# Filling the block-diagonal keys by transfers instead of masked copies, in a four-layer transformer kernel on one core

## The chip, the cores and the metric

The kernel runs on one core of one Trainium2 chip. Its time is the device time of one launch in microseconds (us); the figure that counts is the median of several runs. The engines are named as in the profile: PE multiplies matrices, PEld loads its weights, DVE, ACT and POOL work elementwise, SP issues DMAs.

## The reference, cut to what matters

There are 128 sequences of 64 tokens with 128 channels, a condition vector for each sequence and a context of 64 tokens for each sequence. All is float32. Attention has 16 heads of 8 channels.

```python
x = x + g_sa * (attend(ln(x) * (1 + sc) + sh) @ sa_proj_w + b)     # layer 0, self attention:  L0s
x = x + attend(q=ln(x), kv=context) @ ca_proj_w + b                # layer 0, cross attention: L0c
x = x + g_ff * mlp(ln(x) * (1 + sc_ff) + sh_ff)                    # MLP of layer 0
x = x + attend(q=ada_ln(x, c), kv=ada_ln(context, c)) @ Wp + bp    # layer 1, cross attention: L1c
x = x + gate_a * (attend(ln(x) * (1 + s) + t) @ W_proj + b)        # layer 2, self attention:  L2s
x = x + attend(q=ln(x), kv=ln(context)) @ W_cproj + b              # layer 2, cross attention: L2c
x = x + gate_m * mlp(...)                                          # MLP of layer 2
x = x + sigmoid(...) * (sum_e prob_e * expert_e(...) @ out_w + b)  # layer 3: one head, router, three experts
# attend: per sequence and head softmax(q k^T / sqrt(8)) v, with q, k, v projections and biases
```

## The kernel before, in words

The sequences are cut into 16 groups of 8 (512 tokens). The x of all groups stays in SBUF. Five attention layers of 16 groups each, 80 groups in all, go through one software pipeline, `attend`; MLPs and layer 3 have their own.

**Heads inside one matmul.** `prepare` (line 386) makes for each group qT and kT, both 128 channels x 512 tokens. A head has 8 channels, and PE multiplies 32 rows at a time: 4 heads share 32 rows. So that one query row block meets the keys of each head alone, the keys are spread into `kbd` (128 x 4 x 8 x 64): slice j holds the keys of the j-th head of each four and zeros elsewhere. Lines 443 to 446 make it with four POOL instructions, kT times a 0/1 mask column. `scores` (line 468) multiplies qT with kbd into `sc`, takes the maximum (`mx`, L485) and subtracts it (`e`, L487), both on DVE. `turned` (line 493) transposes on PE (`pp`, L503), and ACT takes the exponential on the way out (`eT`, L507).

**Values, sums and o.** `vbd` holds for each pair of heads the 16 value columns of the pair and two columns of ones among 32, so that `weighted` (line 509, `po`, L520) gives values and softmax sums in one multiplication. The result `o` has 128 rows: per 32 rows, 16 of values and two of sums, and two free-axis halves (even and odd pairs).

**finish** (line 530), for each group in four pieces: (0) SP stores the sum rows to DRAM in two DMAs (`sums`), loads them spread over 128 partitions (`rc`), and folds the second half of o into rows 16 to 31 of each 32 with four DMAs (`o<-o`); (1) DVE takes the reciprocal, SP stores it (`recs`), loads the gate tile (`gt`, self attention only, two DMAs from a table in DRAM with 1 KB rows) and the reciprocals repeated over 8 rows each (`rb`, one DMA); (2) POOL multiplies `oT = o * rb` and adds the bias to x; (3) PE projects (`py`, L563), and the result goes into x.

**The order is written by hand.** `step(k)` handles one half group: scores of the present half, `turned` of the last, `weighted` of the one before, with pieces of `prepare` and `finish` between. Each engine runs its instructions in that order, and each waits in place. For group i the keys are made (piece 5 of `prepare`) in the first half of group i-1 and used at the start of group i. `reciprocal`, `recs`, `gt` and `rb` of group i-2 are issued in the first half of group i, before the context load of group i+4 (`c`, L394).

SP issues nearly all DMAs in program order; at the start these are x and all weights.

Of the kernel before, what the change touches and what calls it, by code (L numbers as in the profile page):

```python
# [9 lines left out]
F32 = mybir.dt.float32  # L10
AF = mybir.ActivationFunctionType
ALU = mybir.AluOpType
# [23 lines left out]
for _name, _n in _VECS:  # L36
# [15 lines left out]
}  # L52
_RAW = [
    "x", "cond_1024", "ctx_1024", *_WTS,
    "L0_xcond_ca_proj_b", "L1_xcond_bp", "L2_xcond_b_cproj", "L3_xcond_router_b", "L3_xcond_e_b2",
# [4 lines left out]
def tile_kernel(ctx: ExitStack, tc: tile.TileContext, a: dict, out: bass.AP):  # L60
# [5 lines left out]
    def const(shape, name):  # L66
        return cp.tile(shape, F32, tag=name, name=name)
# [11 lines left out]
    mask = const([P, 4], "mask")  # L79
    nc.scalar.dma_start(mask, a["mask"])  # L80

    w = {}

    def load_weights(prefix, pool=cp):
        for name, (k, n) in _WTS.items():
            if name.startswith(prefix):
                t = pool.tile([P, k, n], F32, tag=name, name=name)
                src = a[name]
                if len(src.shape) == 3:
                    src = src.rearrange("e c n -> (e c) n")  # L90
                nc.sync.dma_start(t, src.rearrange("(k p) n -> p k n", p=P))
                w[name] = t

    xs = [const([P, TT, P], f"x{s}") for s in range(NST)]
# [23 lines left out]

    ident = const([P, P], "ident")
    make_identity(nc, ident)  # L120
    nhalf = const([P, TT], "nhalf")
    G.memset(nhalf, -0.5)

# [37 lines left out]
    def mm(name):  # L161
        return pools[1].tile([P, 512], F32, tag="mm", name=name)
# [4 lines left out]
        Places.ak.tile([P, NB, 8, 32], F32, tag=f"vbd{i}", name=f"vbd{i}", bufs=1) for i in range(2)  # L167
    ]

    def clear(t):  # L170
        G.memset(t, 0.0)
        G.memset(t[0:L, :, :, 16:17], 1.0)
        G.memset(t[L:P, :, :, 17:18], 1.0)


# [2 lines left out]
    condT = const([P, P], "condT")  # L178
    scT = const([P, P], "scT")
    mods = {}  # L180

    def col(name, i=0):
        r = _ROW[name] + i
        return vec[:, r : r + 1]
# [19 lines left out]

    def folded_column(wp, bp, bv, i):
        pb = mm("pb")
        T.matmul(pb[:, 0:1], w[wp][:, 0], col(bv, i), start=True, stop=True)
        t = const([P, 1], "pb_" + wp)
        V.tensor_add(t, pb[:, 0:1], col(bp))
        proj_bias[wp] = t  # L210
# [3 lines left out]
    def gate_table(wmod, wp, i=2, bias=None):  # L214

        table = dp.tile([P, 2, P], F32, tag="gate_" + wp, name="gate_" + wp)
        rows = const([P, 2, P], "gate_rows")
        gb = const([P, P], "gate_bias")
        V.tensor_scalar_mul(gb, mods[wmod][:, i, :], proj_bias[wp] if bias is None else bias)

        def second():
            pg = mm("pg")
            for q, src in enumerate((mods[wmod][:, i, :], gb)):
                T.transpose(pg[:, ts(q, P)], src, ident)
            V.tensor_copy(rows, pg[:, 0 : 2 * P].rearrange("p (i c) -> p i c", i=2))
            nc.sync.dma_start(table, rows)
            gates[wp] = table

        return second

    def folded_row(wp, bp, bv):
        bvs = const([P, P], "bvs")
        V.tensor_copy(bvs, col(bv, 1).broadcast_to([P, P]))

        def second():
            pb = mm("pb")
            T.matmul(pb[:, :P], bvs, w[wp][:, 0], start=True, stop=True)
            V.tensor_add(row_bias[bp], row_bias[bp], pb[:, :P])
            proj_bias[wp] = row_bias[bp]

        return second

    def condition():
        pc = mm("pc")
        T.transpose(pc[:, :P], cond, ident)
        V.tensor_copy(condT, pc[:, :P])
        S.activation(scT, pc[:, :P], AF.Silu)
        pv = mm("pv")
        T.transpose(pv[:, :_NVEC], vec_rows, ident[:_NVEC, :_NVEC])
        V.tensor_copy(vec, pv[:, :_NVEC])  # L250
        V.tensor_scalar_add(vec1, vec, 1.0)

    first_mods = modulations("L0_xcond_adaln_w", "L0_xcond_adaln_b", 6, (1, 4))
# [19 lines left out]
    def gate_tile(pool, s, wp):  # L273

        gt = pool.tile([P, TT, 2, P], F32, tag="gt", name="gt")
        for h in range(2):
            r = gates[wp].rearrange("(s t h) i c -> s h t (i c)", t=TT, h=2)[s, h]
            nc.sync.dma_start(
                gt[ts(h, L)].rearrange("p t i c -> p t (i c)"),
                r.unsqueeze(0).broadcast_to([L, TT, 2 * P]),  # L280
            )
        return gt

# [15 lines left out]
    def by_batch(t):  # L299
        return t.rearrange("p (b l) -> p b l", b=NB)  # L300
# [80 lines left out]

    turn = [0]

    ctxT = dp.tile([NST, P, NT], F32, tag="ctxT", name="ctxT")

    def prepare(pools, at):
# [52 lines left out]
        i = turn[0] % 2  # L439
        turn[0] += 1  # L440
        vbd = vbds[i]
        kbd = pool.tile([P, 4, NB, L], F32, tag="kbd", name="kbd")
        for j in range(4):
            (V if at.get("first") else G).tensor_scalar(  # L444
                kbd[:, j], by_batch(kT), mask[:, j : j + 1], 1.0, ALU.mult, ALU.mult
            )
        yield
        pq = psum.tile([P, 512], F32, tag="mm", name="pq")
        T.matmul(pq, at["wq"], q_in, start=True, stop=True)  # L449
# [11 lines left out]
                    start=True, stop=True,  # L461
                )
        pv4 = pvv.rearrange("p b (i d) -> p b i d", d=HD)
        S.copy(vbd[0:L, :, :, 0:HD], pv4[0:L])
        S.copy(vbd[L:P, :, :, HD : 2 * HD], pv4[L:P])
        at["vbd"] = vbd

    def scores(pools, at, u):
# [61 lines left out]
    def finish(pools, at):  # L530

        pool, psum = pools[:2]
        s, o = at["s"], at["o"]
        cross = at["layer"][2] == "c"

        sums = dp.tile([16, NT], F32, tag="sums", name="sums", bufs=2)
        for j in range(2):
            nc.sync.dma_start(
                sums.rearrange("(g i j) t -> j g i t", i=2, j=2)[j], o[16 + j : P : 32, :, :]
            )  # L540
        rc = pool.tile([P, L], F32, tag="rc", name="rc")
        nc.sync.dma_start(rc, sums.rearrange("h (c t) -> (h c) t", t=L))

        for g in range(4):
            nc.sync.dma_start(o[32 * g + 16 : 32 * g + 32, 0, :], o[32 * g : 32 * g + 16, 1, :])
        yield
        V.reciprocal(rc, rc)
        recs = dp.tile([16, NT], F32, tag="recs", name="recs", bufs=2)
        nc.sync.dma_start(recs.rearrange("h (c t) -> (h c) t", t=L), rc)

        if not cross:
            gt = gate_tile(pool, s, at["wp"])
        rb = pool.tile([P, NT], F32, tag="rb", name="rb", bufs=1)
        nc.sync.dma_start(rb, recs.unsqueeze(1).broadcast_to([16, HD, NT]))
        yield
        oT = pool.tile([P, NT], F32, tag="oT", name="oT", bufs=1)
        G.tensor_tensor(oT, o[:, 0, :], rb, ALU.mult)  # L557
        bias = proj_bias[at["wp"]].unsqueeze(1).broadcast_to([P, TT, P]) if cross else gt[:, :, 1, :]
        G.tensor_tensor(xs[s], xs[s], bias, ALU.add)
        yield  # L560
        py = psum.tile([P, TT, P], F32, tag="mm", name="py")
        for t in range(TT):
            T.matmul(py[:, t, :], oT[:, ts(t, P)], w[at["wp"]][:, 0], start=True, stop=True)  # L563
        if cross:
            V.tensor_add(xs[s], xs[s], py)
        else:
            y = pool.tile([P, TT, P], F32, tag="y", name="y")
            V.tensor_tensor(y, py, gt[:, :, 0, :], ALU.mult)
            G.tensor_tensor(xs[s], xs[s], y, ALU.add)

    def attend(pools, ats):
# [5 lines left out]
        def go(gens, i):  # L577
            if 0 <= i < n:
                next(gens[i], None)
# [8 lines left out]
        def step(k, between=(), late=()):  # L588
# [36 lines left out]
    def attention_of(s, layer):  # L625
        if layer[2] == "s":
            wmod, wqkv, bqkv, wp = {
                "L0s": ("L0_xcond_adaln_w", "L0_xcond_qkv_w", "L0_xcond_qkv_b", "L0_xcond_sa_proj_w"),
                "L2s": ("L2_xcond_W_mod", "L2_xcond_W_qkv", "L2_xcond_b_qkv", "L2_xcond_W_proj"),
            }[layer]  # L630
            m = w[wqkv][:, 0]
            return dict(
                s=s, layer=layer, wmod=wmod, wp=wp, wq=m[:, 0:P], bq=col(bqkv, 0),
                wk=m[:, P : 2 * P], bk=col(bqkv, 1), wv=m[:, 2 * P : 3 * P],
            )
        wq, bq, wkv, bkv, wp = {
            "L0c": (
# [8 lines left out]
        }[layer]  # L646
        m = w[wkv][:, 0]
        return dict(
            s=s, layer=layer, wp=wp, wq=w[wq][:, 0], bq=col(bq), wk=m[:, 0:P], bk=col(bkv, 0),
            wv=m[:, P : 2 * P],  # L650
        )

# [537 lines left out]
    def stages():  # L1190
# [134 lines left out]
```

## Time and profile before

| what | value |
|---|---|
| median of three runs | 1625.87 us (1625.56 to 1628.92) |
| the profiled execution | 1626.31 us, its span 1624.5 us |
| granted TensorE clock | 0.997 |
| PE, DVE, ACT, POOL busy | 97%, 76%, 64%, 66% of the span |
| POOL making kbd, L444 | 316 instructions of 690 ns, 212.4 us |

The span is what the profiler saw of the program; 1.8 us lie around it. A group of instructions is named by its line, engine, operation and "out<-in"; for a DMA, the time that the engine's queue took to issue it is shown, not its transfer. "SPq" is SP's queue of DMA issues, "idle before" is the time that an engine stood still just before an instruction, and "<-" names what ended it.

### The profile page before, as it was taken

To read this page: it belongs to the slowest core of one execution; us is meant where nothing else is said; L and a number is where in the kernel's file an instruction comes from. 1 tells how busy PE (TensorE), PEld (TensorE's weight loads), DVE (VectorE), ACT (ScalarE), POOL (GpSimd) and SP (SyncE) were. 2 spreads that over 40 slices of the span, in tenths; PEclk is the share of its full clock that TensorE was granted. 3 is DMA by queue.
4 is the path that set the end of the run, shared out by engine and by line. 5 is a ranking of instruction groups with operands and counts; after the bars stand their busy time and mean duration, and the time that the engine had idled before them with its cause. 6 is when DMAs were issued, how large, how long until landed. Compare 5 with 4: busy or idle time off the path is not lost.

```text
span 1624.5 us, 64028 instructions
## 1 busy us (share of the span) xinstructions
PE 1573.8 (97%) x27842; PEld 1086.8 (67%) x27842; DVE 1240.4 (76%) x1566; ACT 1035.5 (64%) x1710; POOL 1072.5 (66%) x1786
## 2 busy tenths in 40 slices
PE   6999999998999899999999999998999999999998
PEld 4676777776544577776777777776777566666665
DVE  7898998898555688899899889896443566666666
ACT  5788777776433678878888888886334544444443
POOL 6687787766888789887787876775875333333322
PEclk9999999999999999999999999999999999999999
DMA  8334453332111022211334432222533111111100
GB/s 209 85 82 99 107 127 92 83 83 72 55 36 55 16 63 61 72 44 50 90 82 102 104 88 73 62 56 59 130 81 76 31 39 37 40 33 36 34 12 19
DMA packets 146775, 112.65 MB, mean 69 GB/s; under 512 B 36357, under 2 KB 125247, under 8 KB 146495
## 3 DMA queue, kind: packets, MB, share of 16 engines
q1 hardware_dynamic: 146288, 108.53, 26.1%
q8 instruction: 219, 3.59, 0.9%
q14 instruction: 61, 0.50, 0.1%
q10 hardware_dynamic: 207, 0.03, 0.0%
HBM read 83.99 MB, written 14.02 MB: 60 GB/s over the span
## 4 chain that ended last, share of the span: by engine, by line
PE 83%; DVE 12%; ACT 3%; issue 1%; DMA 0%; SPq 0%; DVEq 0%
PE sc L478 10%; PE pp L503 9%; PE po L520 7%; PE ph L693 7%; PE ph L1080 6%; PE ph L1081 6%; DVE e L487 6%; DVE mx L485 6%; PE po L1111 5%; PE psT L342 5%; PE pk L436 5%; PE py L563 4%; PE py L709 4%; PE py L699 3%; PE pvv L459 3%; PE pq L449 3%
## 5 line engine op out<-in xcount | busy, mean ns | idle before, releaser
L507 ACT ACTIVATE eT<-pp 128x1024 f32<-128x1024 f32 x320 | 329.7, 1030 | 160.8 <-PE pp L503 160.7
L485 DVE TENSOR_REDUCE mx<-sc 128x32 f32<-128x2048 f32 x160 | 366.6, 2291 | 83.6 <-PE sc L478 83.6
L487 DVE TENSOR_TENSOR e<-sc,mx 128x2048 f32<-128x2048 f32 x160 | 366.6, 2291 | 5.4
L503 PEld LDWEIGHTS pp<-ident,e 64*128 64x128 f32 x5120 | 183.9, 138 | 140.1 <-ACT eT L507 44.7
L503 PE MATMUL pp<-ident,e 64*128 64x64 f32 x5120 | 227.7, 229 | 7.2 <-DVE e L487 4.7
L444 POOL TENSOR_SCALAR kbd<-kT,mask 128x512 f32<-128x512 f32 x316 | 212.4, 690 | 31.3 <-ACT kT L438 28.3
L372 POOL TENSOR_SCALAR xn<-x,nmu,rs 128x128 f32<-128x128 f32 x508 | 223.6, 453 | 13.3
L557 POOL TENSOR_TENSOR oT<-o,rb 128x512 f32<-128x512 f32 x80 | 102.1, 1276 | 163.5 <-DMA rb<-recs 62.9
L478 PE MATMUL sc<-kbd,qT 32*64 32x256 f32 x5120 | 179.2, 387 | 16.6 <-DVE e L487 15.6
L694 ACT ACTIVATE h<-ph,vec 128x512 f32<-128x512 f32 x128 | 87.3, 687 | 149.9 <-PE ph L693 149.7
L520 PE MATMUL po<-eT,vbd 128*32 128x64 f32 x10240 | 178.1, 221 | 1.4 <-issue 1.3
L1087 ACT ACTIVATE h<-h 128x512 f32<-128x512 f32 x112 | 70.6, 630 | 149.8 <-DVE h L1083 130.9
L520 PEld LDWEIGHTS po<-eT,vbd 128*32 128x32 f32 x10240 | 151.3, 110 | 14.4 <-issue 2.0
L330 POOL TENSOR_TENSOR rs<-rs,nhalf 128x4 f32<-128x4 f32 x128 | 130.2, 1017 | 10.7
L478 PEld LDWEIGHTS sc<-kbd,qT 32*64 32x64 f32 x5120 | 97.7, 131 | 53.0 <-issue 19.6
L1083 DVE TENSOR_TENSOR h<-ph,ab 128x512 f32<-128x512 f32 x112 | 76.9, 687 | 62.6 <-PE ph L1081 62.5
L1116 DVE SCALAR_TENSOR_TENSOR acc<-po,pr,acc 128x128 f32<-128x128 f32 x192 | 67.2, 350 | 44.1 <-PE po L1111 39.6
L1080 PE MATMUL ph<-nx,w 128*128 128x512 f32 x192 | 100.7, 607 | 0.0
L528 ACT COPY o<-po 128x512 f32<-128x512 f32 x160 | 95.7, 598 | 5.1 <-PE po L520 2.0
L1081 PE MATMUL ph<-u,w_ev 128*128 128x512 f32 x192 | 98.9, 597 | 0.0
L1111 PEld LDWEIGHTS po<-w_2o,h 128*128 128x128 f32 x768 | 92.1, 192 | 8.7 <-issue 8.4
L1104 POOL TENSOR_SCALAR g<-g 128x512 f32<-128x512 f32 x16 | 9.9, 622 | 132.1 <-ACT g L1103 132.1
(259 smaller groups left out, 2868.5 us busy)
## 6 DMA issues: line engine op xcount, KB each, us to landing
rb<-recs SPq DMA_DIRECT2D x80, 256.0 KB
c<-in_ctx_dram SPq DMA_DIRECT2D x64, 256.0 KB
o<-o SPq DMA_DIRECT2D x320, 32.0 KB
gt<-gate_L_xcond_sa_proj_w SPq DMA_DIRECT2D x32, 256.0 KB
gt<-gate_L_xcond_W_proj SPq DMA_DIRECT2D x32, 256.0 KB
gt<-gate_L_xcond_W_mlp SPq DMA_DIRECT2D x32, 256.0 KB
x<-in_x_dram SPq DMA_DIRECT2D x16, 256.0 KB
ctxT<-cm SPq DMA_DIRECT2D x16, 256.0 KB
```

Of the source, the lines that this page charges most:

```text
L330: G.tensor_tensor(rs, rs, nhalf, ALU.pow)
L372: engine.tensor_scalar(xn[:, t, :], src[:, t, :], nmu[:, t : t + 1], rs[:, t : t + 1], ALU.add, ALU.mult)
L444: (V if at.get("first") else G).tensor_scalar(kbd[:, j], by_batch(kT), mask[:, j : j + 1], 1.0, ALU.mult, ALU.mult)
L478: T.matmul(sc[ts(h, L), g, ts(t2, 256)], qT[ts(g, 32), ts(b, L)], kbd[ts(g, 32), :, b, :], start=True, stop=True,)
L485: V.tensor_reduce(mx, sc.rearrange("p g (m k) -> p (g m) k", k=L), AX.X, ALU.max)
L487: V.tensor_tensor(e, sc.rearrange("p g (m k) -> p (g m) k", k=L), mx.unsqueeze(2).broadcast_to([P, 32, L]), ALU.subtract,)
L503: T.transpose(pp[:, h, ts(4 * g2 + 2 * i + t2, L)], e6[ts(h, L), 2 * gg + g2, t2, i], ident[ts(h, L), ts(h, L)],)
L507: S.activation(eT[:, gg], pp, AF.Exp, scale=HD ** -0.5)
L520: T.matmul(po[ts(g, 32), i, ts(2 * t2 + h, L)], at["vbd"][:, 4 * u + 2 * t2 + h, 2 * g + i, :], e7[:, g // 2, h, g % 2, i, t2, :], start=T ...
L1080: T.matmul(ps, wn, d["nx"], start=True, stop=False)
L1081: T.matmul(ps, we, d["u"], start=False, stop=True)
L1111: T.matmul(po[:, ex, :], d[q][:, ts(t, P)], k3["w_2o"][:, q, :], start=r == 0, stop=r == 1)
```

## The change

Heads that share 32 rows are interleaved: channel row d*4+j holds channel d of head j, where j*8+d did. Then slice j of kbd is every fourth row. The two kbd tiles are kept for the whole attention; the first two fillings use the mask and write zeros too, and the other 78 are four DMAs each of 32 rows of 2 KB, issued by POOL (`spread`). The query and key weights are put into the new order on the chip: for layer 0's self attention by DVE before its first group, for the others by POOL, one weight after each odd step in L0s (`reorder`). Bias columns come in three orders (`vec`, `vecp`, `vecv`); the mask is made from the identity matrix instead of loaded.

In vbd the two heads of a pair are interleaved, and columns 1 and 17 are the ones. Values then stand in the even rows of o, the sums in rows 1 and 17 of each 32: one DMA stores them, and one DMA (64 rows) folds the second half of o into the odd rows. The projection weights are loaded with rows in that order, two DMAs each. `rb` becomes two DMAs, one for even and one for odd rows. The gate table is stored so that a row of the gate tile is 4 KB in one piece. `finish` has one more piece: `recs` is stored in one, `gt` and `rb` are loaded in the next, and the context load of group i+4 stands between; the keys' piece of group i+1 stands ahead of both.

```diff
@@ prepare
-        kbd = pool.tile([P, 4, NB, L], F32, tag="kbd", name="kbd")
-        for j in range(4):
-            (V if at.get("first") else G).tensor_scalar(
-                kbd[:, j], by_batch(kT), mask[:, j : j + 1], 1.0, ALU.mult, ALU.mult
-            )
+        kbd = kbds[i]
+        by_mask = turn[0] <= 2
+        if by_mask:
...
+        else:
+            spread(kbd, kT)
...
-        S.copy(vbd[0:L, :, :, 0:HD], pv4[0:L])
-        S.copy(vbd[L:P, :, :, HD : 2 * HD], pv4[L:P])
+        S.copy(vbd[0:L, :, :, 0 : 2 * HD : 2], pv4[0:L])
+        S.copy(vbd[L:P, :, :, 2 * HD : 4 * HD : 2], pv4[L:P])
@@ new
+    def spread(kbd, kT):
+        for j in range(4):
+            G.dma_start(kbd[j:P:4, j].rearrange("p b l -> p (b l)"), kT[j:P:4, :])
+    def reorder(engine, name, n):
+        for i in range(n):
+            t = const([P, P], "gate_bias")
+            cols = w[name][:, 0, ts(i, P)]
+            engine.tensor_copy(t.rearrange("p (g d j) -> p g d j", d=HD, j=4), by_element(cols))
+            engine.tensor_copy(cols, t)
@@ finish
-        for j in range(2):
-            nc.sync.dma_start(
-                sums.rearrange("(g i j) t -> j g i t", i=2, j=2)[j], o[16 + j : P : 32, :, :]
-            )
+        nc.sync.dma_start(sums.rearrange("(m i) t -> m i t", i=2), o[1:P:16, :, :])
...
-        for g in range(4):
-            nc.sync.dma_start(o[32 * g + 16 : 32 * g + 32, 0, :], o[32 * g : 32 * g + 16, 1, :])
+        nc.sync.dma_start(o[1:P:2, 0, :], o[0:P:2, 1, :])
...
         nc.sync.dma_start(recs.rearrange("h (c t) -> (h c) t", t=L), rc)
+        yield
         if not cross:
             gt = gate_tile(pool, s, at["wp"])
...
-        nc.sync.dma_start(rb, recs.unsqueeze(1).broadcast_to([16, HD, NT]))
+        for i in range(2):
+            r = recs.rearrange("(m i) t -> i m t", i=2)[i]
+            nc.sync.dma_start(rb[i:P:2, :], r.unsqueeze(1).broadcast_to([8, HD, NT]))
@@ step, first half of a group
+                go(prep, i + 1)
                 go(fin, i - 2)
                 go(prep, i + 4)
-                go(prep, i + 1)
+                go(fin, i - 2)
                 go(fin, i - 3)
@@ gate_tile (h is one of two 64-row halves)
-                r.unsqueeze(0).broadcast_to([L, TT, 2 * P]),
+                r.unsqueeze(0).broadcast_to([L, TT * 2 * P]),
@@ stages
         condition()
+        reorder(V, "L0_xcond_qkv_w", 2)
...
-        for f in steps_1[6:-n]:
+        for i, f in enumerate(steps_1[6:-n]):
             f()
+            if i % 2 and i // 2 < len(names):
+                reorder(G, *names[i // 2])
```

More of the change, by code (lines that the diff above doesn't have):

```diff
@@ L52 @@
 }
+_TURNED = (
+    "L0_xcond_sa_proj_w", "L0_xcond_ca_proj_w", "L1_xcond_Wp", "L2_xcond_W_proj",
+    "L2_xcond_W_cproj",
+)
 _RAW = [
@@ L78, in tile_kernel @@
     nc.scalar.dma_start(vec_rows, a["vecs"])
-    mask = const([P, 4], "mask")
-    nc.scalar.dma_start(mask, a["mask"])
     w = {}
@@ L90, in load_weights @@
                     src = src.rearrange("e c n -> (e c) n")
-                nc.sync.dma_start(t, src.rearrange("(k p) n -> p k n", p=P))
+                if name in _TURNED:
+                    of = src.rearrange("(g i r) n -> i g r n", i=2, r=2 * HD)
+                    for i in range(2):
+                        nc.sync.dma_start(t[i:P:2, 0, :], of[i])
+                else:
+                    nc.sync.dma_start(t, src.rearrange("(k p) n -> p k n", p=P))
                 w[name] = t
@@ L120, in tile_kernel @@
     make_identity(nc, ident)
+    mask = const([P, 4], "mask")
+    V.tensor_reduce(mask, ident.rearrange("p (q j) -> p j q", j=4), AX.X, ALU.add)
     nhalf = const([P, TT], "nhalf")
@@ L168, in tile_kernel @@
     ]
+    kbds = [
+        Places.ak.tile([P, 4, NB, L], F32, tag=f"kbd{i}", name=f"kbd{i}", bufs=1) for i in range(2)
+    ]
     def clear(t):
         G.memset(t, 0.0)
-        G.memset(t[0:L, :, :, 16:17], 1.0)
+        G.memset(t[0:L, :, :, 1:2], 1.0)
         G.memset(t[L:P, :, :, 17:18], 1.0)
@@ L180, in tile_kernel, with by_element, colp, colv @@
     mods = {}
+    vecp = const([P, _NVEC], "vecp")
+    vecv = const([P, _NVEC], "vecv")
+    def by_element(t):
+        return t.rearrange("p (g j d) -> p g d j", j=4, d=HD)
+    def colp(name, i=0):
+        r = _ROW[name] + i
+        return vecp[:, r : r + 1]
+    def colv(name, i=0):
+        r = _ROW[name] + i
+        return vecv[:, r : r + 1]
     def col(name, i=0):
@@ L206, in folded_column @@
         pb = mm("pb")
-        T.matmul(pb[:, 0:1], w[wp][:, 0], col(bv, i), start=True, stop=True)
+        T.matmul(pb[:, 0:1], w[wp][:, 0], colv(bv, i), start=True, stop=True)
         t = const([P, 1], "pb_" + wp)
@@ L225, in second @@
             V.tensor_copy(rows, pg[:, 0 : 2 * P].rearrange("p (i c) -> p i c", i=2))
-            nc.sync.dma_start(table, rows)
+            for h in range(2):
+                nc.sync.dma_start(
+                    table.rearrange("(s h t) i c -> h s t (i c)", t=TT, h=2)[h],
+                    rows[h:P:2].rearrange("p i c -> p (i c)"),
+                )
             gates[wp] = table
@@ L232, in folded_row @@
         bvs = const([P, P], "bvs")
-        V.tensor_copy(bvs, col(bv, 1).broadcast_to([P, P]))
+        V.tensor_copy(bvs, colv(bv, 1).broadcast_to([P, P]))
         def second():
@@ L241, in folded_row @@
         return second
-    def condition():
+    def reorder(engine, name, n):
[4 more added lines that the diff above has]
+            engine.tensor_copy(cols, t)
+    def condition():
+        vec_rows_p = const([P, P], "gate_bias")[:_NVEC]
+        vec_rows_v = const([P, 2, P], "gate_rows")[:_NVEC, 0, :]
+        V.tensor_copy(
+            vec_rows_p.rearrange("p (g d j) -> p g d j", d=HD, j=4), by_element(vec_rows)
+        )
+        V.tensor_copy(
+            vec_rows_v.rearrange("p (g r i) -> p g r i", r=2 * HD, i=2),
+            vec_rows.rearrange("p (g i r) -> p g r i", r=2 * HD, i=2),
+        )
         pc = mm("pc")
@@ L249, in condition @@
         T.transpose(pv[:, :_NVEC], vec_rows, ident[:_NVEC, :_NVEC])
+        T.transpose(pv[:, P : P + _NVEC], vec_rows_p, ident[:_NVEC, :_NVEC])
+        T.transpose(pv[:, 2 * P : 2 * P + _NVEC], vec_rows_v, ident[:_NVEC, :_NVEC])
         V.tensor_copy(vec, pv[:, :_NVEC])
+        V.tensor_copy(vecp, pv[:, P : P + _NVEC])
+        V.tensor_copy(vecv, pv[:, 2 * P : 2 * P + _NVEC])
         V.tensor_scalar_add(vec1, vec, 1.0)
@@ L276, in gate_tile @@
         for h in range(2):
-            r = gates[wp].rearrange("(s t h) i c -> s h t (i c)", t=TT, h=2)[s, h]
+            r = gates[wp].rearrange("(s h t) i c -> s h (t i c)", t=TT, h=2)[s, h]
             nc.sync.dma_start(
-                gt[ts(h, L)].rearrange("p t i c -> p t (i c)"),
-                r.unsqueeze(0).broadcast_to([L, TT, 2 * P]),
+                gt[ts(h, L)].rearrange("p t i c -> p (t i c)"),
+                r.unsqueeze(0).broadcast_to([L, TT * 2 * P]),
             )
@@ L441, in prepare @@
         vbd = vbds[i]
-        kbd = pool.tile([P, 4, NB, L], F32, tag="kbd", name="kbd")
-        for j in range(4):
-            (V if at.get("first") else G).tensor_scalar(
-                kbd[:, j], by_batch(kT), mask[:, j : j + 1], 1.0, ALU.mult, ALU.mult
-            )
+        kbd = kbds[i]
+        by_mask = turn[0] <= 2
+        if by_mask:
+            for j in range(4):
+                (V if at.get("first") else G).tensor_scalar(
+                    kbd[:, j], by_batch(kT), mask[:, j : j + 1], 1.0, ALU.mult, ALU.mult
+                )
+        else:
+            spread(kbd, kT)
         yield
@@ L553, in finish @@
         rb = pool.tile([P, NT], F32, tag="rb", name="rb", bufs=1)
-        nc.sync.dma_start(rb, recs.unsqueeze(1).broadcast_to([16, HD, NT]))
+        for i in range(2):
+            r = recs.rearrange("(m i) t -> i m t", i=2)[i]
+            nc.sync.dma_start(rb[i:P:2, :], r.unsqueeze(1).broadcast_to([8, HD, NT]))
         yield
@@ L632, in attention_of @@
             return dict(
-                s=s, layer=layer, wmod=wmod, wp=wp, wq=m[:, 0:P], bq=col(bqkv, 0),
-                wk=m[:, P : 2 * P], bk=col(bqkv, 1), wv=m[:, 2 * P : 3 * P],
+                s=s, layer=layer, wmod=wmod, wp=wp, wq=m[:, 0:P], bq=colp(bqkv, 0),
+                wk=m[:, P : 2 * P], bk=colp(bqkv, 1), wv=m[:, 2 * P : 3 * P],
             )
@@ L648, in attention_of @@
         return dict(
-            s=s, layer=layer, wp=wp, wq=w[wq][:, 0], bq=col(bq), wk=m[:, 0:P], bk=col(bkv, 0),
+            s=s, layer=layer, wp=wp, wq=w[wq][:, 0], bq=colp(bq), wk=m[:, 0:P], bk=colp(bkv, 0),
             wv=m[:, P : 2 * P],
@@ L1251, in stages @@
         n = last + 2 + len(heads_0)
-        for f in steps_1[6:-n]:
-            f()
+        names = (
+            ("L0_xcond_q_w", 1), ("L0_xcond_kv_w", 1), ("L1_xcond_Wq", 1), ("L1_xcond_Wkv", 1),
+            ("L2_xcond_W_qkv", 2), ("L2_xcond_W_qc", 1), ("L2_xcond_W_kvc", 1),
+        )
+        for i, f in enumerate(steps_1[6:-n]):
+            f()
+            if i % 2 and i // 2 < len(names):
+                reorder(G, *names[i // 2])
         for s in range(2):
```

## The prediction

> **What bounds the kernel now.** I read the busy time of the engines by layer first (from 17 to 1118 us lie the five attention layers, the only stage that the change touches in its steady state).
>
> ```profile
> core 0: us, PE busy (x) PEld busy (x) DVE busy (x) ACT busy (x) POOL busy (x), PEclk, DMA share, GB/s
> 17.00:205.00 188.00, 178.47 (x4599) 129.17 (x4601) 169.18 (x131) 150.94 (x276) 141.40 (x217) 1.00 0.44 106
> 211.00:398.00 187.00, 184.42 (x4751) 134.93 (x4752) 168.42 (x126) 133.56 (x181) 132.89 (x203) 1.00 0.33 89
> 545.00:733.00 188.00, 180.11 (x4578) 129.77 (x4576) 167.81 (x112) 148.50 (x274) 158.34 (x261) 1.00 0.21 54
> ```
>
> Rows: L0s, L0c, L1c. A group takes 11.9 to 12.25 us in every layer (distance of the `mx` of successive groups). PE is idle 9.5, 2.6 and 7.9 us per layer. POOL is busy 8.6 to 9.4 us of a group's 12, so has 3 to spare, but in L1c 158 of 188 us, 10.2 of 12.2. Then the waits: who made PE and POOL stand still?
>
> ```profile
> POOL oT L557 <- DMA rb<-recs: 62.9, 21, 8.7
> POOL kbd L444 <- ACT kT L438: 28.3, 24, 4.0
> PE sc L478 <- DVE e L487: 15.6, 37, 2.9
> PEld py L563 <- POOL oT L557: 13.9, 22, 1.6
> ```
>
> The columns are total us, times, longest. PE itself never waits for kbd; what it waits for is DVE. The POOL wait in the last line holds back a weight load, which overlaps matmuls. Last the timeline of one group in L1c, where POOL is fullest (start, duration, engine):
>
> ```profile
> 607.57 0.69 ACT L438 ACTIVATE kT<-pk,vec 128x512 f32<-128x512 f32 x1 [0.40 <-PE pk L436]
> 608.44 1.02 POOL L330 TENSOR_TENSOR rs<-rs,nhalf 128x4 f32<-128x4 f32 x1
> 609.54 2.69 POOL L444 TENSOR_SCALAR kbd<-kT,mask 128x512 f32<-128x512 f32 x4
> 612.50 1.73 POOL L372 TENSOR_SCALAR xn<-x,nmu,rs 128x128 f32<-128x128 f32 x4
> 614.32 1.16 SPq L538 DMA_DIRECT2D sums<-o  x2
> 615.34 0.42 PEld L342 LDWEIGHTS psT<-ident,xn 128*128 128x128 f32 x4
> 615.93 0.66 PEld L478 LDWEIGHTS sc<-kbd,qT 32*64 32x64 f32 x32 [0.17 <-issue]
> 616.81 1.04 POOL L348 TENSOR_TENSOR xm<-xm,mod_L_xcond_Wss_q 128x512 f32<-128x512 f32 x1 [0.86 <-DVE xm L347]
> 617.33 0.32 SPq L542 DMA_DIRECT2D rc<-sums  x1
> ```
>
> The keys are done at 612.23 and used at 615.93: 3.7 us of cover, 6.4 from the start of the first of the four. The critical chain of this stretch has no POOL piece. So attention is bound by PE, and no work that leaves POOL shortens it; the change can gain at most a part of PE's idle time, and can lose wherever a cover is used up.
>
> **The change part by part.**
>
> *Keys by DMA.* Removed: 78 x 4 x 0.69 us of POOL. Added: 78 x 4 issues on POOL, in the same place of its queue (the order of instructions shows rs, rs, the four, then x, nmu, xn as before), waiting for the same kT. No row shows a DMA issued by POOL. Nearest below: SP's issue of the same kind of copy, SBUF to SBUF in 2 KB rows, where a row of the timeline has `o<-o` x4 in 2.46 us, 0.62 each. [...] I take d = 1.0 per issue, next to that row. The transfer after it: from the end of the last `sums` issue at 615.48 to the `rc` that waits for it at 617.33 are 1.85 us, in the group before 1.37; with `rb` 2.9. I take 1.7. The keys are then ready 4 x 1.0 + 1.7 = 5.7 us after POOL gets to them. Read off the timeline of each layer (medians), there are 6.7 us in L0s, 7.3 in L0c, 6.4 in L1c, 6.8 in L2s, 7.3 in L2c. Covered everywhere, by 0.7 to 1.6.
>
> [...]
>
> *What stands behind on POOL.* With 4.0 for 2.69, `nmu`, `xn` and `cn` come 1.3 us later. In L1c `xn` ends at 614.23 and PE takes it up at 615.34: 1.1 us of cover, so 0.2 us a group, 16 x 0.2 = 3 us. Bounds: nothing at d = 0.62; at d = 1.5 POOL needs 3.3 more, 2.2 beyond the cover, 35 us. In the other layers POOL has 3 us free per group, and I book nothing.
>
> *PE's wait for keys.* The first matmul of a group waits for four DMA semaphores where one of POOL was; that is one more wait instruction on PE, and the wait instruction ahead of `sc` takes 0.05 us in the trace. 78 x 0.05 = 4 us if none lies under the wait for `e`; the row above has 0.17 idle there. I take 1, bounds 0 and 4.
>
> *Start.* DVE gets, before the statistics of the first x, three small copies and four dependent 128x128 copies that wait for the qkv weights.
>
> ```profile
> 4.13 0.19 DVE L251 TENSOR_SCALAR vec<-vec 128x54 f32<-128x54 f32 x1
> 4.69 0.76 DVE L313 BATCH_NORM_STATS2 mv<-x 128x6 f32<-128x256 f32 x2 [0.37 <-DMA x<-in_x_dram]
> 7.16 1.12 DVE L372 TENSOR_SCALAR xn<-x,nmu,rs 128x128 f32<-128x128 f32 x4 [1.71 <-POOL nmu L369]
> 8.91 2.10 DVE L357 TENSOR_SCALAR xm<-psT,mod_L_xcond_adaln_w 128x64 f32<-128x64 f32 x8
> 15.72 1.12 PE L478 MATMUL sc<-kbd,qT 32*64 32x256 f32 x32 [0.87 <-DVE kbd L444]
> ```
>
> The packets of the qkv weights (1536 B rows) end at 5.7 us, a waiter goes on some 0.5 later; four copies by the row of `condT` (128x128, 0.29) are 1.2. The statistics begin at 7.4 instead of 4.7, and all to the first `sc` hangs on them: 2.6 us later. Bounds 1.5 (quicker copies) and 3.5. Nothing later gives it back, as PE is bound from there on.
>
> *Reordering by POOL in L0s.* Nine pairs of 128x128 copies, by the `xn` row (0.45 for such a tile) 0.9 us a pair, ahead of the keys in eight groups or fewer. Cover there 6.7 - 5.7 = 1.0, so only the weight with two pairs sticks out: 1 us. At d = 1.5 all do: 15 us. Once, the first DMA of POOL may cost start-up; no row shows it, 0 to 6, taken 0.
>
> *finish.* SP issues 8 instead of 11 DMAs a group in self attention, but SP mostly waits for others (137.7 us for `rc`). Only the last input of `oT` counts, and that is `rb`. Its issue becomes two, 0.55 us more; the 4 KB rows of `gt` ahead of it may bring that back, since in L2s `gt` and `rb` together keep the DMA engines full for 3 us. In the cross layers the context load passes ahead of `rb`, 0.6 us of SP's queue, but SP waited there for `recs` anyway. `py` starts 0.9 us (L0s), 1.4 (L2s), 2.4 (L0c, L2c) after `oT` ends. Booked at 0; bounds 0 and 0.5 x 32 self-attention groups = 16 us. [...]
>
> *ACT and the rest.* vbd is written with a step of two, the same 512 elements a lane in 0.58 us; nothing booked, bounds 0 and 0.1 x 80 us, which ACT's idle time hides. The MLPs and layer 3 keep their work.
>
> Sum: 2.6 + 3 + 1 + 1 = 7.6 us on the profiled 1626.3, 1633.9. That execution lies 0.44 above the median of 1625.87, so the forecast is **1633.5 us**, 0.5% slower; what a measurement can tell from no change here is about 0.2%, 3.3 us.
>
> **The rivals.** *Keys late in every group.* If POOL's issue takes 1.5 us, the keys are ready after 7.7 us; they come late by 1.0 (L0s), 0.4, 1.3, 0.9 and 0.4 us, 16 x 4.0 = 64 us, and with 2.6 of the start and 4 of waits some 1696. It decides from d = 1.2 (L1c) on. For it: nothing measured speaks for a cheap issue, four in a row on an in-order engine. Against: the cover is real in all layers.
>
> *Faster.* POOL gets lighter and passes that on. Place: POOL's queue in L0s, L1c and L2s, where PE's idle time is 9.5 + 7.9 + 5.7 = 23 us; half of it back less 2.6 of the start gives 1617. It decides at d below 0.67, the price of a masked copy. Against it: PE's idle time names `e` and ACT, not POOL.
>
> *No change to be told.* d near 0.7, no wait added, and only the start is paid: 1628.5.
>
> **How the numbers follow.** The forecast (covered keys, small losses) 0.50; keys late 0.20; no change 0.13; faster 0.17. Slower is 0.50 + 0.20 = 0.70. The range goes from 1619, within the faster case, so that about 0.1 of chance lies below, to 1672, that is d = 1.35, with 0.1 of the late case above.
>
> **What would show it.** Right: POOL's four issues near 1 us each; `sc` in a group's first half still waiting for `e`; first `mx` at 19.5 instead of 16.9; L1c 0.2 us a group longer, the other layers within 0.1. Wrong: PE waiting for `kbd` transfers (rival one), or PE's idle time in L0s, L1c and L2s falling by 10 us (rival two), or `py` waiting for `oT` in self attention, which my zero would have missed.

## The result, and the profile after

| | before | after |
|---|---|---|
| median of four runs each, same chip | 1627.39 us (1625.56 to 1630.28) | 1654.19 us (1652.1 to 1656.79) |
| the profiled execution | 1626.31 us | 1653.28 us |
| its span | 1624.5 us | 1651.5 us |
| granted TensorE clock | 0.997 | 0.991 |
| PE busy, from the page | 1573.8 us | 1582.5 us |

The ratio is 1.0164, interval 1.014 to 1.0187. The forecast was 7.6 us more; the span grew by 27.0. The sign was right, the size was not.

First the busy time by layer after the change (L0s, L0c, L1c, L2s, each from its first `mx` to its last, on whole us):

```profile
core 0: us, PE busy (x) PEld busy (x) DVE busy (x) ACT busy (x) POOL busy (x), PEclk, DMA share, GB/s
19.00:214.00 195.00, 179.64 (x4578) 130.24 (x4570) 168.39 (x130) 152.24 (x276) 140.46 (x232) 0.99 0.43 119
222.00:411.00 189.00, 185.11 (x4754) 135.08 (x4754) 168.68 (x125) 135.15 (x181) 126.71 (x203) 1.00 0.35 109
559.00:749.00 190.00, 182.72 (x4588) 131.07 (x4589) 168.90 (x115) 150.67 (x275) 152.79 (x263) 0.99 0.23 75
754.00:944.00 190.00, 182.03 (x4734) 132.84 (x4714) 168.27 (x125) 152.47 (x275) 138.94 (x216) 0.99 0.36 104
```

PE idles 15.4 us in L0s (9.5 before), 8.0 in L2s (5.7 before), but 7.3 in L1c, where the forecast had seen the tightest queue. Most of the loss lies in self attention: from a layer's first `mx` to the next layer's, L0s takes 9.0 us more and L2s 6.9, 15.9 of the 27.0 us. By the distance of the `mx` of successive groups, L0s goes from 12.094 to 12.612 us a group, L2s from 11.957 to 12.201, L0c from 12.090 to 12.215, L1c from 12.179 to 12.234, L2c from 12.086 to 12.151; the step from the last `mx` of L2s to the first of L2c alone is 3.4 us longer. The waits name what is new:

```profile
POOL oT L622 <- DMA rb<-recs: 122.9, 40, 5.7
POOL kbd L444 <- ACT kT L500: 22.6, 19, 4.3
PEld py L628 <- POOL oT L622: 21.1, 32, 1.2
PE sc L544 <- DMA kbd<-kT: 15.4, 12, 3.1
PE sc L544 <- DVE e L553: 7.1, 7, 2.9
```

PE now waits for the key transfers: 12 times, 15.4 us in all, in 12 of 78 groups. POOL's wait for `rb` has doubled from 62.9 us. Both could be the cause, since a late `rb` holds POOL at `oT` and the keys' issues stand behind `oT`. What the four issues and their transfers cost is in the answer for the tile kbd and in the costliest groups:

```profile
L444 POOL DMA_DIRECT2D kbd<-kT x312 | 172.6, 555 | 32.4 <-ACT kT L500 22.6
```

```profile
DMA to landing us min/median/max: 1.7/2.7/6.1
```

An issue takes 0.555 us, not the 1.0 assumed; four take 2.2 us, less than the 2.69 of the four masked copies. A landing is counted from the start of its issue: it takes 1.7 us only at its shortest, and up to 6.1.

**One stall, read in order.** The timeline of a group of L2s (rows left out are of other steps):

```profile
899.46 1.28 POOL L622 TENSOR_TENSOR oT<-o,rb 128x512 f32<-128x512 f32 x1 [2.97 <-DMA rb<-recs]
...
901.11 0.69 ACT L500 ACTIVATE kT<-pk,vecp 128x512 f32<-128x512 f32 x1 [0.40 <-PE pk L498]
...
903.35 2.20 POOL L444 DMA_DIRECT2D kbd<-kT  x4
...
903.91 0.44 SPq L456 DMA_DIRECT2D c<-in_ctx_dram  x1
904.45 1.15 SPq L334 DMA_DIRECT2D gt<-gate_L_xcond_W_proj  x2
905.71 1.27 SPq L619 DMA_DIRECT2D rb<-recs  x2
...
911.25 1.30 PE L544 MATMUL sc<-kbd,qT 32*64 32x256 f32 x32 [2.29 <-DMA kbd<-kT]
```

kT is done at 901.80. `oT` came late (after `rb`), so POOL reaches the keys at 903.35, 1.55 us after kT. The last issue ends at 905.55. PE is ready for the keys at 911.25 - 2.29 = 908.96; with 1.7 us after the last issue they would have been there at 907.3. But the last of the four landed 6.1 us after the start of its issue, at 911.1, and PE went on at 911.25. Between 903.9 and 907.0 SP issues a context load of 256 KB, a gate tile of two transfers of 256 KB and two halves of `rb` of 128 KB; with the keys' 256 KB that is 1.28 MB. The windows of one us show what that does (last two columns: share of the 16 DMA engines that is busy, GB/s):

```profile
905.00:906.00 1.00, 0.93 (x64) 0.77 (x56) 1.00 (x1) 1.00 (x5) 0.98 (x3) 1.00 0.40 112
906.00:907.00 1.00, 0.89 (x2) 0.30 (x2) 0.97 (x2) 1.00 (x3) 1.00 (x2) 1.00 1.15 394
907.00:908.00 1.00, 1.00 (x23) 0.77 (x24) 1.00 (x1) 1.00 (x3) 0.90 (x4) 1.00 1.05 217
908.00:909.00 1.00, 0.95 (x32) 0.81 (x28) 1.00 (x2) 0.94 (x2) 0.86 (x3) 1.00 1.06 213
```

From 906 to 909 the engines are full (1.05 to 1.15 by these rows), and with the packets of both queues: of the time of the 16 engines in these 3 us, SP's (q1) take 84.0% and POOL's (q0) 22.1%. The landing is 6.1 us here, against 1.7 at the shortest.

**Which group is hit.** The order in time decides a good part of it. Take the 26 groups whose keys are issued while a self-attention group loads its gate tile (groups 3 to 15 and 51 to 63). In 10 of them the first `gt` issue started 1.65 us or more after POOL's first key issue; there the four transfers had landed 2.9 to 5.0 us after that first key issue. In the other 16 it came closer, or just before; there it took 2.9 to 7.8 us, in 9 of them over 5.7. Three runs below that do not bring the load forward (e2, e4, e6) show the same: none of the 29 groups with the later `gt` took over 5.1 us, and 18 of the 49 with the closer one took over 5.7.

**The sum of what was lost.** PE's idle time, span less busy, goes from 50.7 to 69.0 us: +18.3. The waits for keys are 15.4 of it, but they partly take the place of others: PE's waits of `sc` for `e` fall from 15.6 to 7.1. The later start is 2.5 (first `mx` at 19.48 instead of 16.94). And 3.4 us lie behind the last matmul, from which the kernel before needs 4.5 us to the end of the span and the changed one 7.9. There POOL runs an instruction named DRAIN; the rows of line 1321 before and 1394 after have (duration in ns min/median/max):

```profile
L1321 POOLq DRAIN  x3: 39/78/556, 1620.4 to 1624.3; - x3
L1394 POOLq DRAIN  x3: 34/244/6292, 1644.0 to 1651.2; - x3
```

The long one takes 6.29 us in every profile here whose keys are made by DMA and 0.56 in every one without. So it comes with POOL's DMAs; what it waits for, no row shows. The other 5.5 us of idle time are small waits, 2.0 of them of `py` for `oT`.

PE's busy time grows by 8.7 us, with 27844 matmuls for 27842. The profile has stretches in which the granted clock is 0.5: three before, eight after. The last of each begins behind the last matmul; the others are 3.4 us long. That leaves five more with work in them; as an estimate, half of 3.4 us lost in each, 5 x 1.7 = 8.5 us. Two windows of the trace after the change, each about such a stretch (the clock is the column after the busy times):

```profile
912.00:915.60 3.60, 3.60 (x97) 2.84 (x82) 2.97 (x2) 1.05 (x2) 3.43 (x4) 0.53 0.16 50
953.00:956.40 3.40, 3.40 (x101) 2.59 (x82) 2.54 (x2) 1.02 (x1) 2.96 (x4) 0.51 0.15 51
```

Together: 18.3 + 8.7 = 27.0 us. This split holds for the profiled execution alone: another of the four had a clock of 0.997 and still took 1652.1 us, so what the clock did not cost there was lost in another way.

### The profile page after: what moved, and what is told of

Same layout as the page of the kernel before. It is cut to its first block, busy times and chain, and to the rows that moved or that the text cites. A ratio compares the mean times of both kernels' runs of the same rounds, so it can differ in the third digit from the quotient of the medians.

```text
span 1651.5 us, 63956 instructions
## 1 busy us (share of the span) xinstructions
PE 1582.5 (96%) x27844; PEld 1093.6 (66%) x27844; DVE 1242.5 (75%) x1575; ACT 1044.5 (63%) x1710; POOL 1045.7 (63%) x1802
## 4 chain that ended last, share of the span: by engine, by line
PE 73%; DMA 8%; ACT 6%; DVE 5%; POOL 5%; issue 2%; SPq 1%; POOLq 0%; DVEq 0%
PE pp L569 8%; PE sc L544 7%; PE ph L759 7%; PE ph L1146 6%; PE ph L1147 6%; PE po L586 5%; PE po L1177 5%; PE pvv L525 4%; PE pq L515 4%; PE pk L498 4%; PE psT L398 3%; DMA rb<-recs 3%; PE py L775 3%; DMA kbd<-kT 3%; PE py L628 3%; PE py L765 3%
## 5 line engine op out<-in xcount | busy, mean ns | idle before, releaser
L544 PE MATMUL sc<-kbd,qT 32*64 32x256 f32 x5120 | 180.8, 389 | 28.6 <-DMA kbd<-kT 15.4
L444 POOL DMA_DIRECT2D kbd<-kT x312 | 172.6, 555 | 32.4 <-ACT kT L500 22.6
L1177 PE MATMUL po<-w_2o,h 128*128 128x128 f32 x768 | 95.8, 275 | 0.0
```

Source lines behind the costliest of these rows:

```text
L444: G.dma_start(kbd[j:P:4, j].rearrange("p b l -> p (b l)"), kT[j:P:4, :])
L544: T.matmul(sc[ts(h, L), g, ts(t2, 256)], qT[ts(g, 32), ts(b, L)], kbd[ts(g, 32), :, b, :], start=True, stop=True,)
L1177: T.matmul(po[:, ex, :], d[q][:, ts(t, P)], k3["w_2o"][:, q, :], start=r == 0, stop=r == 1)
```

## The experiments

Three theories. A: the key transfers share the DMA engines with the gate tile, the context load and `rb`, and land late. B: `rb` itself, in two halves, comes late, holds POOL at `oT`, and so the keys. C: only the small terms of the forecast. Ratios are to the kernel before on the same chip; its medians were 1626.71 us in the first four runs, 1625.84 in the next four, 1626.48 in the last two. The layer figures are from the profiled executions.

**The keys by mask again (e1_masks).** Everything else of the change stays.

```diff
-        by_mask = turn[0] <= 2
+        by_mask = True
```

> All 80 fillings of the kept key tiles by POOL's mask instructions, as the changed kernel does the first two; the interleaved order, the even rows of o, the two rb transfers, the gate rows of 4 KB and the order of the steps stay. Theory A (the four key transfers share the DMA engines with gt, rb and the context load issued in the same few us and land late, so PE waits for keys): the PE waits for kbd, 15.4 us in all, go, and with them the spells at half clock; 5 to 10 us above the kernel before remain (start 2.6 us, rb late). Theory B (rb on fewer DMA engines comes late and holds POOL at oT, so whatever fills the keys starts late): masks start as late as the transfers do, PE waits for py stay, 12 to 25 us above before. Theory C (the prediction's small terms, POOL's queue and the wait instructions): within 5 us of the kernel before.

1630.81 us (1627.02 to 1634.75), ratio 1.0026 (1.001 to 1.0041). The key part of the change costs 23 of 27 us, the 3.4 us at the end among them. `rb` is late all the same:

```profile
POOL oT L622 <- DMA rb<-recs: 121.0, 49, 7.7
```

So 121 us of POOL waiting for `rb` cost next to nothing by themselves. B falls as the cause on its own: it is at most what makes the keys' issue late.

**The key part alone on the kernel before (e2_keys_alone).** Interleaved heads, `spread` and `reorder` stay; vbd, sums, halves, `rb`, gates and the order of pieces are those of before. Against the changed kernel, in excerpts:

```diff
-        nc.sync.dma_start(o[1:P:2, 0, :], o[0:P:2, 1, :])
+        for g in range(4):
+            nc.sync.dma_start(o[32 * g + 16 : 32 * g + 32, 0, :], o[32 * g : 32 * g + 16, 1, :])
...
-                go(prep, i + 1)
                 go(fin, i - 2)
                 go(prep, i + 4)
-                go(fin, i - 2)
+                go(prep, i + 1)
```

> The kernel before with the key part alone: interleaved key and query weights, kept key tiles, four transfers by POOL; o, sums, the single rb transfer, the gate rows of 1 KB and the order of the steps as before. Theory A: key transfers still meet gt and rb, so PE waits for kbd stay at 10 us or more and the time is 12 to 30 us above before. Theory B: rb is back on one transfer, POOL is not held longer than before, 3 to 6 us above before (start 2.6 us). Theory C: the same 3 to 6 us.

1648.39 us (1641.99 to 1655.66), ratio 1.0131 (1.0091 to 1.0171). `oT` waits 55.3 us for `rb`, less than before the change, and still `sc` waits for `kbd`: 9 times, 9.9 us, worst in L0s (12.573 us a group). Its profiled execution is 19.4 us longer than before: 9.9 of waits for keys (those for `e` fall by 7.5), 2.4 of start (first `mx` at 19.4), 3.0 behind the last matmul and 5.6 more of PE busy time are the large pieces. The order of the pieces is that of before, so the waits do not need the new order.

**The gate tile out of the keys' way (e3_gt_early).** The gate tile is loaded two pieces of `finish` earlier, behind `o<-o`; its bytes and their number stay.

```diff
         nc.sync.dma_start(o[1:P:2, 0, :], o[0:P:2, 1, :])
+        if not cross:
+            gt = gate_tile(pool, s, at["wp"])
         yield
...
-        if not cross:
-            gt = gate_tile(pool, s, at["wp"])
         rb = pool.tile([P, NT], F32, tag="rb", name="rb", bufs=1)
```

> The changed kernel with the gate tile loaded two steps of finish earlier, right behind the o<-o transfer, so that its 512 KB are not in flight with the keys. Theory A: PE waits for kbd in L0s and L2s go except where the context load is in flight too; 5 to 15 us below the changed kernel. Theory B: rb is no longer queued behind gt and lands about 1.5 us earlier, POOL is held less; also below, by 5 to 10 us, and POOL's wait for rb falls from 122.9 us to under 80. Theory C: no change.

1635.24 us (1632.87 to 1636.79), ratio 1.005 (1.0034 to 1.0066): 19 us come back by moving two DMA issues. The waits of this kernel:

```profile
POOL oT L622 <- DMA rb<-recs: 127.6, 46, 7.2
PE sc L544 <- DMA kbd<-kT: 0.4, 2, 0.2
```

`rb` is no earlier, the keys are in time. The longest landing falls from 6.1 to 4.9 us, while its median hardly moves (2.7 to 2.6): what counts is the tail.

**rb from 16 source rows (e4_rb16).** `recs` is stored twice (not shown), so that each half of `rb` has 16 source rows instead of 8.

```diff
-            nc.sync.dma_start(rb[i:P:2, :], r.unsqueeze(1).broadcast_to([8, HD, NT]))
+            nc.sync.dma_start(rb[i:P:2, :], r.unsqueeze(1).broadcast_to([16, 4, NT]))
```

> The changed kernel with the reciprocals stored twice (one more DMA of 32 KB), so that each of the two rb transfers reads 16 rows as its slowest dimension. If a transfer runs on as many DMA engines as its slowest dimension allows, rb's packets now keep 16 engines busy instead of 8 and rb lands up to 1 us earlier. Theory A: the key transfers still meet gt and the context load, little is won, 0 to 6 us below the changed kernel. Theory B: POOL's wait for rb falls to near 63 us and 10 to 20 us are won. Theory C: no change, or 1 to 2 us slower by the added DMA.

1660.74 us (1658.49 to 1662.59), ratio 1.021 (1.0183 to 1.0237), slower still, though the intervals just overlap. The wait for `rb` grew to 160.1 us. While `rb` lands, its packets take 84.6% of the 16 engines' time in the kernel before, from 16 source rows (1086.3 to 1087.0 us), and 43.2% after the change, from 8 (1132.2 to 1132.9). In e4 one store more stands ahead of it, so whether the wider transfer by itself is quicker is not told by this run. As a remedy it failed.

**The load put where it was not (e8_gt_cross).** A gate tile is loaded in the cross layers too, and not used there.

```diff
-        if not cross:
-            gt = gate_tile(pool, s, at["wp"])
+        gt = gate_tile(pool, s, "L0_xcond_sa_proj_w" if cross else at["wp"])
```

> The changed kernel with a gate tile also loaded in the three cross-attention layers, ahead of rb as in self attention, and not used there: the suspected load is added where it was absent. Theory A: the keys come late in the cross layers too; PE's waits of sc for kbd appear in L0c, L1c and L2c (there are almost none now), a group there 12.4 to 12.6 us instead of 12.15 to 12.23, so 1666 to 1675. Theory B: oT waits longer for rb by the 1.2 us of two more issues, without waits for kbd; 1654 to 1665. Theory C: SP's queue has room, 1654.

1676.05 us (1673.96 to 1683.98), ratio 1.0318 (1.0296 to 1.034). L0c goes from 12.215 to 12.849 us a group, L2c from 12.151 to 12.681, and PE waits for keys twice as often:

```profile
PE sc L544 <- DMA kbd<-kT: 25.1, 24, 2.1
```

In the cross layers, without the first group of each, it was 1.6 us in L0c, none in L1c and 0.2 in L2c after the change; here it is 4.9, 3.4 and 4.9. That is theory A's wait made to order, though not all of the 22 us is keys: of the 20.6 us by which PE's idle time in the profile grows against the change, they are 9.7. `py` waits more in L0c too (3.9 us for 1.4). The time lies just above A's 1675.

**The context load behind rb (e6_c_late).**

```diff
                 go(fin, i - 2)
-                go(prep, i + 4)
                 go(fin, i - 2)
+                go(prep, i + 4)
```

> The changed kernel with only the context load of group i+4 moved behind the rb issues. Theory A: in L0s and L2s the context load is one of three loads in flight with the keys and the smallest by packet size, and present only in the last groups of a layer whose next layer is a cross layer; the stalls at groups 7, 13, 15, 60 and 63 shrink, those with gt alone stay: 1644 to 1650. Theory B: rb is issued 0.5 us earlier in every layer with a context load, oT and so the keys come earlier: 1640 or less. Theory C: no change, 1654.

1648.67 us (1646.83 to 1652.39), ratio 1.0143 (1.0129 to 1.0158), an interval that overlaps that of the change. The waits for keys halve (8.1 us, 9 times), but `py` now waits 2.7 us for `oT` in L0c and 1.5 in L1c: half a gain and a loss.

**Masks, and a later place for DVE's reordering (e7_masks_start).** On top of e1:

```diff
+        ahead_1(0)
         reorder(V, "L0_xcond_qkv_w", 2)
-        ahead_1(0, 0)
+        ahead_1(0)
```

> The changed kernel with the keys made by the four masked copies in all groups, and the reordering of the qkv weights by DVE behind the statistics of the first x. Against the same kernel without the second edit (1630.8) this measures the start: theory C's 2.6 us there; if DVE's four copies find room while the next operations wait, 1.5 to 2.6 us come back, 1628 to 1629.5, equal to the kernel before. If the start hangs on the qkv weights themselves, nothing comes back: 1631.

1628.47 us (1623.79 to 1631.56), ratio 1.0011 (0.9999 to 1.0022). The first `mx` comes at 17.7 instead of 19.5 us. The four copies now fill DVE's wait for POOL. Against e1's interval the gain is not resolved in the median; what is left of the change without its keys and its start cannot be told from the kernel before.

**Early gate tile, late context, late reordering (e5_early_late).** The edits of e3, e6 and e7's start together, keys by DMA:

```diff
         nc.sync.dma_start(o[1:P:2, 0, :], o[0:P:2, 1, :])
+        if not cross:
+            gt = gate_tile(pool, s, at["wp"])
...
                 go(fin, i - 2)
-                go(prep, i + 4)
                 go(fin, i - 2)
+                go(prep, i + 4)
...
+        ahead_1(0)
         reorder(V, "L0_xcond_qkv_w", 2)
-        ahead_1(0, 0)
+        ahead_1(0)
```

> The changed kernel with three edits of order: the gate tile is loaded in the first piece of finish (after o<-o), the context load of group i+4 stands behind the rb issues, and the reordering of the qkv weights by DVE stands behind the statistics of the first x, not ahead of them. Theory A (the key transfers share the DMA engines with gt, the context load and rb, and land late): the wait of sc for kbd is all but gone, L0s near 12.1 us a group; with the start 1 to 2 us earlier, 1629 to 1633. Theory B (rb itself late): the wait of oT for rb stays near 120 us and so does the time, about 1650. Theory C (only the small terms of the forecast): start alone, about 1652.

1636.34 us (1628.89 to 1637.38), ratio 1.0053 (1.0035 to 1.0071): above what A named. The first `mx` is at 16.9 us and no wait for keys is listed, but L0c is slow (12.425 us a group, 4.3 us of `py` waiting for `oT`), as in e6 with the same move. Against f1 below, which differs by that move alone, the profiled execution is 6.6 us longer; 5.4 of these are PE's busy time.

**Early gate tile and late reordering only (f1_gt_start).** The diff of e5 without its middle part; the context load stays ahead of `rb`.

> The changed kernel with two edits: the gate tile loaded in the first piece of finish, and DVE's reordering of the qkv weights behind the statistics of the first x; the context load stays ahead of rb. The first edit alone gave 1635.2 and the second brought the first mx from 19.5 to 16.9-17.7 us in two other kernels. If the start is a cost of its own, as in the forecast's sum: 2 to 2.6 us less, 1632.6 to 1633.2, still 0.4% above the kernel before. If the profile's half-clock stretches eat it: 1635.

1629.39 us (1626.66 to 1633.4), ratio 1.0019 (1.0005 to 1.0033), the best with keys by DMA, 25 us under the change. The first `mx` is at 17.2 us, 2.4 earlier than e3's 19.6; another 3.8 us against e3 are PE's busy time (1578.7 to 1574.9). The chain that ended last, in the change and here:

```profile
PE 73%; DMA 8%; ACT 6%; DVE 5%; POOL 5%; issue 2%; SPq 1%; POOLq 0%; DVEq 0%
```

```profile
PE 81%; ACT 12%; DVE 4%; DMA 1%; issue 1%; POOL 1%; SPq 0%; POOLq 0%; DVEq 0%
```

DMA falls from 8% to 1% of the chain, though all transfers are still made. What is left above the kernel before is 2.9 us, about the 3.4 that f1 too spends behind the last matmul (its DRAIN takes 6.29 us). No run has the key DMAs without it.

**Only the gate rows of 4 KB, on the kernel before (f2_gate_only).** With the table stored to match:

```diff
-                gt[ts(h, L)].rearrange("p t i c -> p t (i c)"),
-                r.unsqueeze(0).broadcast_to([L, TT, 2 * P]),
+                gt[ts(h, L)].rearrange("p t i c -> p (t i c)"),
+                r.unsqueeze(0).broadcast_to([L, TT * 2 * P]),
```

> The kernel before with only the gate tables stored so that a row of the gate tile is 4 KB in one piece (1 KB pieces before); keys by mask, finish and order as before. If the size of the pieces is what makes gt crowd the other transfers, rb lands otherwise: earlier with quicker gt (the wait of oT for rb under 62.9 us, time 1624 to 1626), or later if 4 KB pieces hold the DMA engines longer ahead of rb (the wait toward 120 us, 1627 to 1629). If gt is paid for elsewhere and rb's two halves are the cause of the longer wait in the changed kernel: no change, 1626.

1624.18 us (1622.3 to 1629.3), ratio 0.9995 (0.9983 to 1.0008): no change. `oT` waits 43.8 us for `rb` (62.9 in the kernel before). So the larger pieces do not crowd `rb` out; they were no harm, nor a measurable gain.

## Why the prediction was right or wrong

*What bounds the kernel: right.* POOL's busy time fell from 66% to 63% of the span and no time was won by it.

*Keys by DMA: d was too high, and the transfer was the mis-sized term.* The step that failed reads "with `rb` 2.9. I take 1.7", and from it "Covered everywhere, by 0.7 to 1.6". It took the landing of a small transfer (two `sums` of 16 KB, with the engines busy to 0.59 from 615.5 to 617.3 us) for one of 256 KB beside three others, with the engines at 1.05 to 1.15. No run shows the 1.0 us of an issue that the sum rests on (4.0 for 2.69, and so the 3 us in L1c), nor the 1.5 of the bounds and of the first rival: the 312 issues took 0.532 us at the shortest, 0.745 at the longest and 0.555 in the mean. With the measured issue, 2.2 + 1.7 = 3.9 us would have left cover to spare; the landing measured 1.7 to 6.1, counted from the start of an issue. From POOL's first issue to the last landing the 78 groups took 2.9 us at the shortest, 4.6 at the median and 8.2 at the longest, and 14 took more than the forecast's 5.7. The cover was read as medians, 6.4 to 7.3 us; in the stall shown, with POOL held at `oT` for 1.55 us after kT, it was 908.96 - 903.35 = 5.6. Together 15.4 us of waits, in 12 groups. By the forecast's own signs ("Wrong: PE waiting for `kbd` transfers") its mechanism failed here. That the time still lies between 1619 and 1672 is luck: the upper end had been set for a slow issue, d = 1.35. The prediction even had the needed fact in hand: in *finish* it says that `gt` and `rb` "keep the DMA engines full for 3 us", and used it for `rb` alone. The keys are issued close to these loads, in the old order (e2) and in the new one, and nothing was booked for it.

*finish, "Booked at 0": nearly right for what it meant.* `oT` waits twice as long for `rb`, but in L0s and L2s the waits of `py` for `oT` go only from 4.2 us to 6.4. e1 keeps all of it and is at 1.0026, 4 us, with the 2.5 of the start among them.

*What stands behind on POOL, 3 us in L1c: wrong.* With four issues shorter than four copies there is no such queue; L1c grew by 0.055 us a group, not 0.2.

*Start, 2.6 us: right, with 2.5 measured.* The changed kernel has the statistics at 7.23 us instead of 4.69 and the first `mx` at 19.48 instead of 16.94:

```profile
6.21 0.28 DVE L283 COPY gate_bias<-L_xcond_qkv_w 128x128 f32<-128x128 f32 x1 [1.55 <-DMA L_xcond_qkv_w<-in_L_xcond_qkv_w_dram]
...
7.23 0.76 DVE L369 BATCH_NORM_STATS2 mv<-x 128x6 f32<-128x256 f32 x2
...
19.48 2.29 DVE L551 TENSOR_REDUCE mx<-sc 128x32 f32<-128x2048 f32 x1 [1.36 <-PE sc L544]
```

It is not a price of the idea: f1 moves the same copies and gets 2.2 us back.

*PE's extra wait and POOL's reordering, 1 us each:* no row shows either apart; they may be among the 5.5 us of small waits. (The kernel makes eight pairs of such copies, not nine.)

*"the first DMA of POOL may cost start-up", taken 0: the price came at the other end.* POOL's first issue took 0.745 us, 0.19 over the mean. The 3.4 us behind the last matmul have no term in the sum.

*The clock: missing.* The sum counted every matmul at its old duration; 8.7 us more of PE busy time were measured, by the estimate above nearly all of it in stretches at half clock.

*The rivals.* "Keys late in every group" named the right wait but a wrong cause: d is 0.555, far under its 1.2, and the keys are late in 12 groups, where other loads are in flight. "Faster" had its condition (d below 0.67) fulfilled and still did not come: PE took nothing from a lighter POOL, as its objection said.

## What to carry to other kernels

A copy turned into a DMA leaves an engine's private time for a shared resource (here POOL's 22.1% and SP's 84.0% of the same engines): size its landing with everything that is issued in the same few microseconds, by bytes, and take the longest landing (6.1 us here), not the shortest (1.7). When such a transfer is late, first move the bulk loads that nobody needs yet; here two issues moved forward by two pieces of `finish` gave 19 of 27 us back. A relieved engine that is not on the chain pays nothing: the best version with keys by DMA is still at 1.0019, about the price of the longer end that POOL's DMAs bring.

## What the runs showed of the hardware that was not expected

A DMA issue on POOL costs 0.555 us for 32 rows of 2 KB, about as much as SP's issues of `o<-o`, also SBUF to SBUF: at the median 0.587 us for 16 rows before the change and 0.523 for 64 rows after it.

POOL's DMAs make the end of the program longer: the DRAIN of 6.29 us instead of 0.56, and 3.4 us more behind the last matmul.

The granted TensorE clock fell to 0.5, for 3.4 us at a time, after short stalls. Seven of the eight stretches in the changed kernel begin between 0.2 us before and 1.3 us after the end of a PE stall of 2.0 to 3.1 us; three of these stalls are waits for keys (2.44, 2.29 and 3.09 us), the other four are stalls of the start of an MLP or of the layer after it, which the kernel before has as well. Not every such stall is followed by one: of those four places, only two have a stretch in the profile before. By this count, as an estimate, 3 x 1.7 = 5.1 of the 8.7 us belong to the waits for keys and 2 x 1.7 = 3.4 to stalls that the kernel before has too; no run here separates them by itself.

Open is why 7 of the 16 groups whose keys and gate tile are issued close together still have their keys within 5.7 us. The context load, in flight at the stall shown, explains only a part: with it moved (e6), PE still waits for keys 9 times instead of 12, though for less time.
